# Four layers over sixteen images: attention scores without their zero blocks, mixing by 64-row halves, a third tile for the exponentials, and an altered order in the search and in the softmax of q

## The chip, the cores and the metric

The kernel runs on one core of one Trainium2 chip. The metric is the device time of one execution in microseconds (us), the median over several runs. All data are float32 unless a tile is named as bf16. The engines are TensorE (PE, with weight loads shown apart as PEld), VectorE (DVE), ScalarE (ACT), GpSimd (POOL) and SyncE (SP, which only issues transfers).

## The reference, cut to what matters

The input is 16 images of 64 x 64 positions with 256 channels. Each layer first normalizes by groups of 8 channels (`_gn`) and adds its result to its input.

```
x = x + L0(gn(x))   # nearest of 1024 codes: argmin of distances, then a lookup
x = x + L1(gn(x))   # per image row of 64 positions: sigmoid(f g^T) h
x = x + L2(gn(x))   # gate = sigmoid(sum_n x2[n] softmax_n(x0[n] x1[m])), times x
x = x + L3(gn(x))   # linear attention, 4 heads of 32, then a layer norm over channels

# L1, the part that the change touches most
f = x Wf + bf ; g = x Wg + bg ; h = x Wh + bh      # 32, 32 and 256 columns
attn = sigmoid(einsum('bhik,bhjk->bhij', f, g))    # 64 x 64 for each image row
out  = einsum('bhij,bhjo->bhio', attn, h)

# L3
q = softmax over the 32 values of a head; k = softmax over the 4096 positions
context = k v^T ; out = (context q) w_out + b_out ; layer norm over 256 channels
```

## The kernel before, in words

An image is 4096 tokens, handled in 8 chunks of 512 (`NCHUNK`, `CW`), a chunk as 4 groups of 128 tokens (`CH`). Every layer is a Python generator that emits instructions and yields a number, its share of progress. At the end of `tile_net_kernel` a list of tasks gives each generator a start and a length on a common axis where one image is one unit; a heap always advances the generator that is due next. So about five images are in flight, each in another layer, and the written order on every engine is a mixture of all layers. The framework adds the waits, and may move an instruction past others of its engine that are not ready. [...]

The stages, with the names used below:

- `stage1` (search): for each group of 128 tokens, ACT writes `nn` (L377), PE makes distances `pd` (L382), DVE adds and takes the maximum (`nd`, L389) and finds its index (`i8`, L394), and POOL issues a gather that adds the code row to the tokens `xc` (L395). `norm(ch)` prepares the next chunk: ACT normalizes (L327) and squares (L330), PE sums (`px`, L336) and turns (`pxt`, L343); `norm_rows(ch)` is one DVE copy `nx2` (L348) that `nn` needs. `back(ch)` turns the gathered tokens (PE, L357), copies them (ACT, L360) and stores them; `tokens` (L321) and `load` (L317) are issues on SP's queue. Before, `norm(ch+1)` comes after group 1 of a chunk, `norm_rows(ch+1)` and `back(ch-1)` after group 2, `tokens` and `load` after group 3.
- `layer1`: `attend(ch)` makes `fg` (PE L465, ACT L472), `h` (PE L476 and L481, ACT L485) and the scores `psc` (PE L494). A group of 128 tokens holds two image rows, so of each 128 x 128 block of scores only the two 64 x 64 blocks on its diagonal are wanted. ACT writes those into `attn`, whose other blocks were set to zero once (L497 tanh, four times for a chunk; L500 scaling, twice). `mix(ch)` multiplies `h` by the 128 x 128 `attn` (PE L509, eight products for a chunk), and DVE adds the result to `xt` (L513).
- `rows2` and `stage2` (exponentials): for 32 groups and two halves, ACT writes `ex`, 128 x 2048 exponentials (L619), and DVE multiplies and sums it in place (L622). `ex` has two tiles. A gate per token follows (L630 to L642); `gate2` applies it.
- `stage3`: for each chunk `pk` (PE L729), its exponential `kx`, `pqv` (PE L751, L755), then transposes `pkt` (L762), the transposes `pq` of the chunk before (`queries`, L717), and the softmax of q: maximum on DVE (L770), subtraction on POOL (L771), exponential on ACT (L772), sum and reciprocal on DVE (L774, L775), product on POOL (L776). After the loop `queries(7)`, then the product of context and `w_out` (PE `pw` L798, DVE `wctx` L800), and eight rounds of output, of which `form` (L817 to L823) reads the queries back from DRAM.

A float32 product appears in the trace as two passes, each with its weight load: a chunk's `mix` is 16 records of PE and 16 of PEld.

Of the kernel before, what the change touches and what calls it, by code (L numbers as in the profile page):

```python
# [16 lines left out]
P = 128  # L17
# [24 lines left out]
def kernel(  # L42
# [82 lines left out]
    def row_tile(name):  # L125
        t = const.tile([P, 2, C], BF16, name=name)
        nc.gpsimd.memset(t, 0.0)
        return t

    h_row, qv_row, x_row = row_tile("h_row"), row_tile("qv_row"), row_tile("x_row")  # L130

    def put_row(dst, v, weight, tag, plus=None):
# [11 lines left out]
        nc.scalar.copy(dst[0:PARTS, :, :], row.unsqueeze(1).to_broadcast([PARTS, 2, C]))  # L144
# [43 lines left out]
    w_src = w_qkv.rearrange("(k p) (s n) -> p k s n", p=P, s=3)  # L188


    gam = s3p.tile([P, C], F32, tag="v2", name="gam", bufs=5)
    nc.scalar.dma_start(out=gam, in_=gamma.rearrange("(o n) -> o n", o=1).to_broadcast([P, C]))

    def centred(src, name):
        t = const.tile([P, 2, C], F32, name=name)
        nc.scalar.dma_start(out=t[:, 0, :], in_=src)
        m = small.tile([P, 1], F32, tag="cen", name=f"cen_{name}")
        nc.vector.tensor_reduce(m, t[:, 0, :], AX.X, ALU.add)
        nc.vector.tensor_scalar(m, m, -1.0 / C, None, ALU.mult)
        nc.vector.tensor_scalar(t[:, 0, :], t[:, 0, :], m, None, ALU.add)  # L200
        nc.vector.tensor_tensor(t[:, 1, :], t[:, 0, :], gam, ALU.mult)
        return t

    wo2 = centred(w_out, "wo2")


    bo2 = centred(b_out.rearrange("(o n) -> o n", o=1).to_broadcast([P, C]), "bo2")
    nc.vector.tensor_scalar(bo2, bo2, float(DH ** 0.5 / HEADS), None, ALU.mult)

# [25 lines left out]

    attn = []
    for n in range(2):
        t = const.tile([P, CH, P], F32, name=f"attn_{n}")
        nc.vector.memset(t, 0.0)
        attn.append(t)  # L240
# [67 lines left out]
    def stage1(b):  # L308
# [63 lines left out]
        for ch in range(NCHUNK):  # L372
            for t in range(CH):
# [27 lines left out]
                if t == 1:  # L401
                    if ch + 1 < NCHUNK:
                        norm(ch + 1)
                        yield 2
                if t == 2:
                    if ch + 1 < NCHUNK:
                        norm_rows(ch + 1)
                    if ch > 0:
                        back(ch - 1)
                        yield 2  # L410
                if t == 3:
                    if ch + 1 < NCHUNK:
                        tokens(ch + 1)
# [10 lines left out]
    def layer1(b):  # L424
# [31 lines left out]
        hs = {}  # L456
        st2 = stats_tile(2, f"st2_{tag}")

        def attend(ch):
# [14 lines left out]
            for t in range(CH):  # L474
# [5 lines left out]
                if t % 2 == 1:  # L480
                    nc.tensor.matmul(  # L481
                        ph[:, t - 1 : t + 1, :], lhsT=ones3, rhs=h_row, start=False, stop=True, skip_group_check=True
# [5 lines left out]
            at = attn[ch % 2]  # L488
            for n in range(2):
                psc = bank(f"psc_{tag}_{ch}_{n}").rearrange("p (t i) -> p t i", i=P)  # L490
                part = slice(n * CK, (n + 1) * CK)
                for t in range(2):
                    cols = slice(t * P, (t + 1) * P)
                    nc.tensor.matmul(psc[:, t, :], lhsT=fg[part, 1, cols], rhs=fg[part, 0, cols], start=True, stop=True)  # L494
                for r in range(2):
                    rows = slice(r * ROW, (r + 1) * ROW)
                    nc.scalar.activation(at[rows, 2 * n : 2 * n + 2, rows], psc[rows, 0:2, rows], AF.Tanh, scale=0.5)  # L497
            for r in range(2):
                rows = slice(r * ROW, (r + 1) * ROW)
                nc.scalar.activation(at[rows, :, rows], at[rows, :, rows], AF.Identity, scale=0.5, bias=half[rows, :])  # L500
# [3 lines left out]
        def mix(ch):  # L504
            at = attn[ch % 2]
            po = wide(f"po_{tag}_{ch}").rearrange("p (k n) -> p k n", k=NK)
            for t in range(CH):
                for k in range(NK):
                    nc.tensor.matmul(  # L509
                        po[:, k, t * P : (t + 1) * P], lhsT=hs[ch][:, t, k * P : (k + 1) * P], rhs=at[:, t, :],  # L510
                        start=True, stop=True,
                    )
            nc.vector.tensor_tensor(xt[ch], po, xt[ch], ALU.add)  # L513
# [80 lines left out]
    def stage2(b, parts=1):  # L594
# [19 lines left out]
        for part in range(parts):  # L614
            those = range(part * NT // parts, (part + 1) * NT // parts)
            for h, (x0b, x2b) in enumerate(halves):
                for T in those:
                    ex = s2p.tile([P, TOK // 2], F32, tag="ex", name=f"ex_{tag}_{h}_{T}", bufs=2)
# [18 lines left out]
            nc.vector.reciprocal(gate, gate)  # L637
            pg = bank(f"pgt_{tag}_{part}")
# [4 lines left out]
            yield 2  # L643
# [46 lines left out]
    def stage3(b):  # L690
# [22 lines left out]
        def queries(ch):  # L713
# [4 lines left out]
            qT = s3p.tile([P, CW], F32, tag="v2", name=f"qT_{tag}_{ch}", bufs=5)  # L718
# [4 lines left out]

        for ch in range(NCHUNK):
            xt = xb.tile([P, NK, CW], F32, tag="xb", name=f"xk_{tag}_{ch}")
            nc.sync.dma_start(out=xt, in_=x3[ch])
            pk = bank(f"pk_{tag}_{ch}")
# [9 lines left out]
            kx = s3p.tile([P, CW], F32, tag="v2", name=f"kx_{tag}_{ch}", bufs=5)  # L737
# [8 lines left out]
            for pr in range(CH // 2):  # L746
# [8 lines left out]
                nc.tensor.matmul(pqv, lhsT=ones3, rhs=qv_row, start=False, stop=True, skip_group_check=True)  # L755
# [7 lines left out]
            ek = s3p.tile([P, CH, P], F32, tag="v2", name=f"ek_{tag}_{ch}", bufs=5)  # L763
# [9 lines left out]
            qd = small.tile([P, CH, HEADS], F32, tag="qd", name=f"qd_{tag}_{ch}")  # L773
# [166 lines left out]
```

## Time and profile before

| | us |
|---|---|
| median of 3 runs | 6005.67 |
| the three runs | 5981.41, 6005.67, 6006.36 |
| the profiled execution, its own time | 5985.76 |
| its span, first to last instruction | 5984.0 |
| PE busy | 5310.6 (89%) |
| DVE busy | 5132.9 (86%) |
| ACT busy | 4756.8 (79%) |
| POOL busy | 1873.7 (31%) |
| mean granted TensorE clock | 0.949 |

The busy time of an engine is the union of its records. PE's records overlap, and an isolated one lasts longer than its slot in a stream, so PE's busy share does not say that it ran at its peak. A wait is put down to the instruction whose signal came last.

### The profile page before, as it was taken

The page shows a single profiled execution, that of the slowest core. Times are in us where ns is not written, and L with a number is a line of the kernel's source. Part 1 is how long each engine was busy: PE and PEld are TensorE (multiplying, and loading weights), DVE is VectorE, ACT ScalarE, POOL GpSimd, SP SyncE. Part 2 cuts the span into 40 slices and gives each one's busy share as a digit, 9 for nine tenths or more (in the row PEclk, how much of TensorE's full clock was granted, in tenths as well). Part 3 has the DMA queues.
Part 4 walks back from the last instruction along what each step waited for, and adds up shares of the span by engine and source line. Part 5 has one row for each costly group of instructions (what it writes and reads, how often), then busy time and mean ns, then how long its engine had stood idle before and what let it go on. Part 6 is the DMA issues. An engine that isn't in the chain of part 4 may idle for free.

```text
span 5984.0 us, 73947 instructions
## 1 busy us (share of the span) xinstructions
PE 5310.6 (89%) x25167; PEld 3208.0 (54%) x25167; DVE 5132.9 (86%) x7270; ACT 4756.8 (79%) x7138; POOL 1873.7 (31%) x1314
## 2 busy tenths in 40 slices
PE   8978798989989899998989989898999989887777
PEld 3535355545556465554646556464655646464445
DVE  6589698899989899898989989898998989888862
ACT  4578597878888797888979788797988879787763
POOL 3222224233332333323333332433333333312231
PEclk9989899999999999999999999999999999998788
DMA  6453645665656657565665746566475655545543
GB/s 185 143 160 112 209 132 186 187 187 158 207 165 201 194 160 227 149 210 163 197 212 156 224 151 207 172 199 203 153 223 160 204 183 172 188 140 176 170 144 111
DMA packets 521359, 1059.10 MB, mean 177 GB/s; under 512 B 52504, under 2 KB 266392, under 8 KB 512792
## 3 DMA queue, kind: packets, MB, share of 16 engines
q1 hardware_dynamic: 406288, 885.11, 44.6%
q0 software_dynamic: 73728, 67.14, 7.8%
q10 hardware_dynamic: 40968, 102.13, 4.5%
q8 instruction: 200, 3.28, 0.2%
q14 instruction: 175, 1.43, 0.1%
HBM read 751.18 MB, written 303.04 MB: 176 GB/s over the span
## 4 chain that ended last, share of the span: by engine, by line
PE 48%; DVE 21%; ACT 15%; issue 7%; DMA 5%; POOL 4%; ACTq 0%; SPq 0%; POOLq 0%; DVEq 0%
PE pd_s L382 16%; DVE ex_s L622 10%; ACT ex_s L619 6%; PE ph_l L476 4%; PE pqv_s L751 4%; PE po_s L849 3%; DVE i_s L394 2%; PE pk_s L729 2%; PE pr_r L567 2%; DVE nd_s L389 2%; PE po_l L509 2%; POOL xc_s L395 2%; PE pvr_s L829 1%; DVE st_s L254 1%; PE pc_s L780 1%
## 5 line engine op out<-in xcount | busy, mean ns | idle before, releaser
L622 DVE CUSTOM_DVE_ANT_0 ex_s<-ex_s,x2b 128x2048 f32<-128x2048 f32 x1024 | 2369.4, 2318 | 135.9 <-ACT ex_s L619 133.5
L619 ACT ACTIVATE ex_s<-x0b,nmax_s,x_r 128x2048 f32<-128x2048 f32 x1024 | 2138.8, 2089 | 64.7 <-DVE num_s L622 55.0
L382 PE MATMUL pd_s<-e,xn_s 128*128 128x512 f32 x4096 | 2013.5, 621 | 87.6 <-DVE m L389 63.8
L395 POOL DMA_INDIRECT xc_s<-in_emb_rows,i_s x512 | 1084.0, 2117 | 1962.9 <-DVE i_s L394 1460.6
L382 PEld LDWEIGHTS pd_s<-e,xn_s 128*128 128x128 f32 x4096 | 750.6, 196 | 830.4 <-issue 655.0
L389 DVE CUSTOM_DVE_ANT_0 nd_s<-pd_s,nn_s 128x1024 f32<-128x1024 f32 x512 | 620.5, 1212 | 114.8 <-PE pd_s L382 85.4
L394 DVE FIND_INDEX8 i_s<-m,nd_s 128x8 uint32<-128x1024 f32 x512 | 623.5, 1218 | 0.0
L377 ACT ACTIVATE nn_s<-ne,nx_s 128x1024 f32<-128x1024 f32 x512 | 585.1, 1145 | 10.6 <-DVE nx_s L348 3.4
L476 PE MATMUL ph_l<-wh_l,xt_l 128*128 128x256 f32 x2048 | 534.6, 396 | 28.6 <-DVE xt_l L513 20.6
L751 PE MATMUL pqv_s<-wqv_s,xk_s 128*128 128x256 f32 x2048 | 491.9, 381 | 2.9 <-ACT xt_s L360 2.9
L476 PEld LDWEIGHTS ph_l<-wh_l,xt_l 128*128 128x128 f32 x2048 | 381.7, 194 | 155.1 <-issue 61.2
L751 PEld LDWEIGHTS pqv_s<-wqv_s,xk_s 128*128 128x128 f32 x2048 | 388.4, 191 | 130.1 <-issue 63.3
L832 POOL TENSOR_TENSOR lrs_s<-lrs_s,mhalf 128x4 f32<-128x4 f32 x128 | 187.6, 1465 | 651.5 <-ACT lrs_s L831 638.0
L849 PE MATMUL po_s<-wctx_s,qo_s 128*128 128x256 f32 x1024 | 329.4, 412 | 63.5 <-ACT y_s L852 59.8
L852 ACT ACTIVATE y_s<-po_s,lrs_s 128x256 f32<-128x256 f32 x512 | 236.0, 470 | 147.5 <-PE po_s L849 104.3
L327 ACT ACTIVATE xn_s<-xt_s,nb_n,s_n 128x512 f32<-128x512 f32 x256 | 202.4, 806 | 108.2 <-DMA xt_s<-in_xT 98.6
L776 POOL TENSOR_TENSOR qv_s<-qv_s,qd_s 128x512 f32<-128x512 f32 x128 | 167.2, 1307 | 385.3 <-DVE qd_s L775 312.8
L509 PE MATMUL po_l<-attn,h_l 128*128 128x128 f32 x2048 | 280.7, 283 | 7.3 <-DVE m L389 5.2
L509 PEld LDWEIGHTS po_l<-attn,h_l 128*128 128x128 f32 x2048 | 259.9, 195 | 45.8 <-issue 22.1
L849 PEld LDWEIGHTS po_s<-wctx_s,qo_s 128*128 128x128 f32 x1024 | 178.0, 199 | 194.5 <-ACT y_s L852 123.9
L729 PE MATMUL pk_s<-xk_s,wk_s 128*128 128x512 f32 x512 | 256.6, 623 | 0.0
L860 DVE TENSOR_TENSOR y_s<-pxo_s,y_s 128x512 f32<-128x512 f32 x256 | 174.1, 683 | 91.4 <-ACT y_s L852 91.3
(197 smaller groups left out, 7707.6 us busy)
## 6 DMA issues: line engine op xcount, KB each, us to landing
xs_s<-in_xT SPq DMA_DIRECT2D x128, 512.0 KB
xt_s<-in_xT SPq DMA_DIRECT2D x128, 512.0 KB
xc_s<-in_x SPq DMA_DIRECT2D x128, 512.0 KB
x_s<-xt_s ACTq DMA_DIRECT2D x128, 512.0 KB
xt_l<-x_s SPq DMA_DIRECT2D x128, 512.0 KB
x_l<-xt_l SPq DMA_DIRECT2D x128, 512.0 KB
xr_r<-x_l SPq DMA_DIRECT2D x128, 512.0 KB
xg_g<-x_l SPq DMA_DIRECT2D x128, 512.0 KB
```

The costliest lines, as they stand in the source:

```text
L377: nc.scalar.activation(nn, ne2, AF.Identity, bias=nx2[ch][:, t : t + 1])
L382: nc.tensor.matmul(pd[:, cols], lhsT=xn[ch][:, k, t * P : (t + 1) * P], rhs=e2[:, k, cols], start=(k == 0), stop=(k == NK - 1),)
L389: nc.vector.tensor_tensor_reduce(out=nd, in0=pd, in1=nn, scale=1.0, scalar=-3.0e38, op0=ALU.add, op1=ALU.max, accum_out=m8[:, 0:1],)
L394: nc.vector.max_index(i8, m8, nd)
L395: nc.gpsimd.indirect_dma_start(out=xc[ch][:, t, :], out_offset=None, in_=emb_rows, in_offset=bass.IndirectOffsetOnAxis(ap=i8[:, 0:1], axis=0),
L476: nc.tensor.matmul(ph[:, t, :], lhsT=X[:, k, t * P : (t + 1) * P], rhs=wh_n[:, k, :], start=(t % 2 == 0 and k == 0), stop=False, skip_grou ...
L509: nc.tensor.matmul(po[:, k, t * P : (t + 1) * P], lhsT=hs[ch][:, t, k * P : (k + 1) * P], rhs=at[:, t, :], start=True, stop=True,)
L619: nc.scalar.activation(ex, x0b, AF.Exp, bias=nmax[:, T : T + 1], scale=x01[:, T, 1:2], accum_out=den[:, h, T : T + 1])
L622: nc.vector.tensor_tensor_reduce(out=ex, in0=ex, in1=x2b, scale=1.0, scalar=0.0, op0=ALU.mult, op1=ALU.add, accum_out=num[:, h, T : T + 1],)
L729: nc.tensor.matmul(pk, lhsT=wk_n[:, k, :], rhs=xt[:, k, :], start=(k == 0), stop=(k == NK - 1))
L751: nc.tensor.matmul(pqv[:, j, :], lhsT=xt[:, k, t * P : (t + 1) * P], rhs=wqv_n[:, k, :], start=(j == 0 and k == 0), stop=False, skip_group ...
L849: nc.tensor.matmul(po[:, j, :], lhsT=qT[:, t * P : (t + 1) * P], rhs=wctx[:, 1, :], start=True, stop=True)
```

## The change

In `layer1`, `attend` makes for each of a chunk's image rows only the 64 x 64 block that is wanted: four products of 32 rows, 128 weight columns and 128 moving columns become eight of 32 rows, 64 weight columns and 64 moving columns, placed so that `psc` holds 128 x 64 for each group. ACT then needs two tanh instructions and one scaling for a chunk. The constant `attn` tiles go; `at` is a rotating tile of 128 x 4 x 64. `mix` multiplies 64 rows at a time: sixteen products of 64 rows, 128 weight columns and 64 moving columns, the two halves of a group one after the other, each half into its own bank of `po`.

`ex` gets a third tile. In `stage1` `back(ch-1)` moves from after group 2 to after group 1, `norm(ch+1)` from 1 to 2, `norm_rows(ch+1)` from 2 to 3. In `stage3` the sum, reciprocal and product of q's softmax become `normalize(ch)`, emitted at the beginning of the next chunk; `queries(7)` moves behind the making of `wctx` and `gram`; `w_out` times gamma is no longer kept, so `pw` has 256 columns and DVE multiplies `wctx` by gamma itself. The row tiles for `ones3` lose their doubled copy (read twice by a broadcast). The `v2` ring goes from 5 to 4 tiles, `wT` and `gram` share the places of `wk_n` and `ctx_bd`. The gate's PE transpose gets a yield ahead of it. `layer1` of the first image gets the length 0.2 in place of 0.35.

```diff
-        nc.scalar.copy(dst[0:PARTS, :, :], row.unsqueeze(1).to_broadcast([PARTS, 2, C]))
+        nc.scalar.copy(dst[0:PARTS, :], row)
...
                 yield 4
-                if t == 1:
-                    if ch + 1 < NCHUNK:
-                        norm(ch + 1)
-                        yield 2
-                if t == 2:
+                if t == 1 and ch > 0:
+                    back(ch - 1)
+                    yield 2
+                if t == 2 and ch + 1 < NCHUNK:
+                    norm(ch + 1)
+                    yield 2
+                if t == 3:
                     if ch + 1 < NCHUNK:
                         norm_rows(ch + 1)
-                    if ch > 0:
-                        back(ch - 1)
-                        yield 2
-                if t == 3:
-                    if ch + 1 < NCHUNK:
                         tokens(ch + 1)
...
-                        ph[:, t - 1 : t + 1, :], lhsT=ones3, rhs=h_row, start=False, stop=True, skip_group_check=True
+                        ph[:, t - 1 : t + 1, :], lhsT=ones3, rhs=twice(h_row), start=False, stop=True, skip_group_check=True
...
-            at = attn[ch % 2]
+            at = ats[ch] = s1p.tile([P, CH, ROW], F32, tag="at", name=f"at_{tag}_{ch}")
+            psc = [bank(f"psc_{tag}_{ch}_{n}").rearrange("p (t i) -> p t i", i=ROW) for n in range(2)]
+            for t in range(2):
+                for r in range(2):
+                    cols = slice(t * P + r * ROW, t * P + (r + 1) * ROW)
+                    for n in range(2):
+                        part = slice(n * CK, (n + 1) * CK)
+                        nc.tensor.matmul(
+                            psc[n][r * ROW : (r + 1) * ROW, t, :], lhsT=fg[part, 1, cols], rhs=fg[part, 0, cols],
+                            start=True, stop=True,
+                        )
             for n in range(2):
-                psc = bank(f"psc_{tag}_{ch}_{n}").rearrange("p (t i) -> p t i", i=P)
-                part = slice(n * CK, (n + 1) * CK)
-                for t in range(2):
-                    cols = slice(t * P, (t + 1) * P)
-                    nc.tensor.matmul(psc[:, t, :], lhsT=fg[part, 1, cols], rhs=fg[part, 0, cols], start=True, stop=True)
-                for r in range(2):
-                    rows = slice(r * ROW, (r + 1) * ROW)
-                    nc.scalar.activation(at[rows, 2 * n : 2 * n + 2, rows], psc[rows, 0:2, rows], AF.Tanh, scale=0.5)
-            for r in range(2):
-                rows = slice(r * ROW, (r + 1) * ROW)
-                nc.scalar.activation(at[rows, :, rows], at[rows, :, rows], AF.Identity, scale=0.5, bias=half[rows, :])
+                nc.scalar.activation(at[:, 2 * n : 2 * n + 2, :], psc[n][:, 0:2, :], AF.Tanh, scale=0.5)
+            nc.scalar.activation(at, at, AF.Identity, scale=0.5, bias=half)
...
-            po = wide(f"po_{tag}_{ch}").rearrange("p (k n) -> p k n", k=NK)
-            for t in range(CH):
-                for k in range(NK):
-                    nc.tensor.matmul(
-                        po[:, k, t * P : (t + 1) * P], lhsT=hs[ch][:, t, k * P : (k + 1) * P], rhs=at[:, t, :],
-                        start=True, stop=True,
-                    )
-            nc.vector.tensor_tensor(xt[ch], po, xt[ch], ALU.add)
+            po = wide(f"po_{tag}_{ch}").rearrange("p (r m i) -> p r m i", r=2, i=ROW)
+            for k in range(NK):
+                for t in range(CH):
+                    for r in range(2):
+                        rows = slice(r * ROW, (r + 1) * ROW)
+                        nc.tensor.matmul(
+                            po[:, r, k * CH + t, :], lhsT=h[rows, t, k * P : (k + 1) * P], rhs=at[rows, t, :],
+                            start=True, stop=True,
+                        )
+            X = xt[ch].rearrange("p k n -> p (k n)").rearrange("p (m r i) -> p m r i", r=2, i=ROW)
+            nc.vector.tensor_tensor(X, po.rearrange("p r m i -> p m r i"), X, ALU.add)
...
-                    ex = s2p.tile([P, TOK // 2], F32, tag="ex", name=f"ex_{tag}_{h}_{T}", bufs=2)
+                    ex = s2p.tile([P, TOK // 2], F32, tag="ex", name=f"ex_{tag}_{h}_{T}", bufs=3)
...
+            yield 1
             pg = bank(f"pgt_{tag}_{part}")
...
-            yield 2
+            yield 1
...
+        def normalize(ch):
+            q4 = qvs[ch][:, :, 0, :].rearrange("p t (h d) -> p t h d", d=DH)
+            qd = small.tile([P, CH, HEADS], F32, tag="qd", name=f"qd_{tag}_{ch}")
+            nc.vector.tensor_reduce(qd, q4, AX.X, ALU.add)
+            nc.vector.reciprocal(qd, qd)
+            nc.gpsimd.tensor_tensor(q4, q4, qd.unsqueeze(3).to_broadcast([P, CH, HEADS, DH]), ALU.mult)
+
         for ch in range(NCHUNK):
...
+            if ch > 0:
+                normalize(ch - 1)
             pk = bank(f"pk_{tag}_{ch}")
...
             nc.scalar.activation(qv[:, :, 0, :], qv[:, :, 0, :], AF.Exp)
-            qd = small.tile([P, CH, HEADS], F32, tag="qd", name=f"qd_{tag}_{ch}")
-            nc.vector.tensor_reduce(qd, q4, AX.X, ALU.add)
-            nc.vector.reciprocal(qd, qd)
-            nc.gpsimd.tensor_tensor(q4, q4, qd.unsqueeze(3).to_broadcast([P, CH, HEADS, DH]), ALU.mult)
...
-        queries(NCHUNK - 1)
+        normalize(NCHUNK - 1)
...
-            nc.tensor.matmul(pw, lhsT=ctx_bd, rhs=wo2, start=True, stop=True)
+            nc.tensor.matmul(pw[:, :C], lhsT=ctx_bd, rhs=wo, start=True, stop=True)
...
-            nc.vector.scalar_tensor_tensor(
-                wctx, pw.rearrange("p (s c) -> p s c", s=2), rk, bo2, op0=ALU.mult, op1=ALU.add
-            )
+            nc.vector.scalar_tensor_tensor(wctx[:, 0, :], pw[:, :C], rk, bo, op0=ALU.mult, op1=ALU.add)
+            nc.vector.tensor_tensor(wctx[:, 1, :], wctx[:, 0, :], gam, ALU.mult)
...
-            wT = wts.tile([P, NK, P], F32, tag="wT", name=f"wT_{tag}")
+            wT = wts.tile([P, NK, P], F32, tag="wk_n", name=f"wT_{tag}")
...
-            gram = wts.tile([P, P], F32, tag="gram", name=f"gram_{tag}")
+            gram = wts.tile([P, P], F32, tag="ctx_bd", name=f"gram_{tag}")
...
         yield 4
+        queries(NCHUNK - 1)
...
-        end = task("layer1", b + 1 + LAG1, LEN1 if left and b else 0.35, layer1(b), 88)
+        end = task("layer1", b + 1 + LAG1, (LEN1 if b else 0.2) if left else 0.35, layer1(b), 88)
```

## The prediction

> **What bounds the kernel now.** I read the page's busy shares first, then the windows, then who waited for whom, then the groups by form, and last the timeline around `psc` and `mix`.
>
> ```profile
> PE 5310.6 (89%) x25167; PEld 3208.0 (54%) x25167; DVE 5132.9 (86%) x7270; ACT 4756.8 (79%) x7138; POOL 1873.7 (31%) x1314
> ...
> 1200.00:4800.00 3600.00, 3305.20 (x15983) 2011.54 (x15984) 3259.26 (x4593) 3021.05 (x4535) 1185.51 (x819) 0.97 0.60 187
> 2782.00:3134.00 352.00, 325.08 (x1574) 199.09 (x1574) 318.13 (x453) 296.19 (x445) 117.49 (x82) 0.96 0.60 188
> ```
>
> The columns of the windows are PE, PEld, DVE, ACT, POOL. In the steady part an image takes 352 us: the same stall of PE (`pg_n`) recurs at 2782, 3134 and 3486 us. Of these PE is busy 325, DVE 318, ACT 296. So PE is the tightest, DVE is 7 us behind it, and no engine is full: PE's 27 us of gaps are what a change of order can win, and PE's 325 are a floor for the period.
>
> ```profile
> ACT qv_s L772 <- POOL qv_s L771: 89.8, 48, 4.4
> DVE ex_s L622 <- ACT ex_s L619: 82.3, 65, 3.2
> DVE qd_s L774 <- ACT qv_s L772: 47.0, 35, 3.0
> PE pg_n L264 <- DVE qd_s L775: 43.9, 10, 5.6
> ACT ex_s L619 <- DVE num_s L622: 29.9, 22, 2.4
> PE po_s L849 <- ACT y_s L852: 28.9, 36, 2.2
> PE px_s L336 <- ACT sq_s L330: 27.3, 14, 3.2
> PE pq_s L717 <- POOL qv_s L776: 23.4, 7, 3.8
> ```
>
> These are the waits of 1200 to 4800 us (us in total, times, longest). PE's gaps there are 3600 - 3305 = 295 us; over all PE's waits, half of that (149) ends on ACT, 113 on DVE, 23 on POOL. The longest, `pg_n`, is the statistics at the end of a search (transposes, ACT copy, DVE statistics behind an `ex` of 2.3 us): the reciprocal L775 is only the last DVE instruction ahead of it, and the change leaves that chain.
>
> **The change part by part.** All sums are against the profiled execution, 5985.8 us (span 5984.0). It lies 20 below the median of 6005.67; I carry the difference over to the median unchanged.
>
> *1. `mix` in halves, PE.*
>
> ```profile
> L509 PE MATMUL po_l<-attn,h_l 128*128 128x128 f32 x2048 | 280.7, 283 | 7.3 <-DVE m L389 5.2 <-ACT h_l L485 1.5 <-ACT attn L500 0.6
> ...
> 3016.25 0.95 PE L829 MATMUL pvr_s<-one,qz_s 128*128 128x1 f32 x8
> 3017.13 0.72 PE L494 MATMUL psc_l<-fg_l 32*128 32x128 f32 x8
> 3019.19 1.95 PE L509 MATMUL po_l<-attn,h_l 128*128 128x128 f32 x16
> ...
> 498.69 1.02 PE L382 MATMUL pd_s<-e,xn_s 128*128 128x512 f32 x2
> 499.64 0.72 PE L494 MATMUL psc_l<-fg_l 32*128 32x128 f32 x8
> 500.29 1.12 PE L382 MATMUL pd_s<-e,xn_s 128*128 128x512 f32 x2
> ```
>
> A `mix` now is 16 passes: (1.95 - 0.28 for the last one's length) / 15 = 0.112 us each. L829 moves one column only and still takes (0.95 - 0.25) / 7 = 0.10 a pass: the load of 128 weight columns alone fills the slot. The change doubles the passes to 32 and keeps 128 weight columns; only the moving columns halve. `psc` shows what the two halves can do: its eight passes use two row groups of 32 and take 0.72, that is four slots of 0.112 and the last length of 0.27, so two row groups load and multiply side by side. Then 32 passes are 16 pairs of 0.112 = 1.79 us, as before. The Trainium skill ("TensorEngine Tiling (Array Packing)", Theoretical Speedup) gives up to twofold for a contraction of at most 64: by that rule 0.9 us would go from each of 128 mixes, -115 us. The L829 row speaks against it, and so I take nothing.
>
> The same page (Key Properties) says that a switch of the tiling mode drains TensorE, which speaks against the change. The row: from 498.69, two slots of L382 (0.43 each, the start-to-start time within L382) end at 499.55, `psc` starts at 499.64; its four pairs would need 0.45 and the next L382 starts after 0.65; and within that one the second pass follows after 0.53, not 0.43. The excursion costs 0.09 + 0.20 + 0.10 = 0.39 us beyond its slots. A `mix` had no such switch and gets one: 128 x 0.39 = +50 us of PE. Without the rule and the row it would be 0. Bounds: if loads of 64 rows took half, 128 x (0.39 - 0.9) = -65; if the halves ran one after the other, 128 x (0.39 + 1.79) = +279. I take +50, since `psc` is the same construction.
>
> *2. Other PE work.* `psc` gets 64 weight and 64 moving columns and four tiles of the array; its four rounds of 0.112 may halve: 128 x -0.22 = -29, or 0; I take -25 (the column-tiled L465 runs four tiles side by side as well). `pw` loses 256 of 512 columns: 2 passes x 0.215 x 16 images = -7. PE in all: +50 - 25 - 7 = +18, of which 92% (PE's busy share, 1200 to 4800) reach the time: **+16**.
>
> *3. ACT.*
>
> ```profile
> L497 ACT ACTIVATE attn<-psc_l 64x128 f32<-64x128 f32 x512 | 138.2, 270 | 70.6 <-PE psc_l L494 59.3 <-issue 2.8
> L500 ACT ACTIVATE attn<-attn,half 64x256 f32<-64x256 f32 x256 | 129.5, 506 | 6.3
> ```
>
> The elements of a partition stay the same, the instructions halve: a chunk saves 2 x 270 + 506 = 1046 ns, 128 chunks 134 us; 48 row copies of 3x512 (565 ns) become 3x256 (356 ns, row L142), -10. ACT loses 144 of 4757 us. ACT isn't the bound: it idles 579 of 3600 us. What it gives is that fewer waits end on it. Scaled from 3600 us to all images (352 us each, 16) PE's waits on ACT are 230. A fall from 84% to 81% busy should shorten its queueing by about a fifth: **-45**; bounds 0 (DVE, as full, takes its place) and -144.
>
> *4. Third `ex` tile.* No instruction is added. ACT's waits for DVE at L619 are 55 us in all, DVE's for ACT at L622 133. A pair costs DVE 2318 + 82 and ACT 2089 + 190 ns, so on average DVE is the slower and the buffer smooths only. **-12**, bounds 0 and -60. When ACT runs ahead, other ACT work behind those exponentials comes later by up to 2.3 us; that is in the bound.
>
> *5. q's softmax.* DVE stands 70.6 us for L772's exponential at L774 (57 times); a yield later it is done. POOL's product moves as well, and PE's `pq`, which waits for it 51.7 us already, gets one yield less. The steady 3.8 us of each image are of the first chunk: POOL stands 9.2 us after its all-reduce (row `POOL qv_s L771 <- issue`), three gathers queue, then L776. That remains. **-12**; bounds -50 and +50. `queries(7)` behind `wctx` costs nothing elsewhere: its transposes were ahead of `pw` and are now ahead of the first `form`, which in steady state has three other layers beside it; uncovered, at the end, 0.7 PE and 0.6 ACT and a store.
>
> *6. Order in the search.* SP's load L317 waits 401 us in all for the store of the chunk two before (94 times, up to 8.4); ACT waits 98.6 at L327 for such loads. With `back` a group earlier the store is done when SP comes to L317, and L321, the tokens (421 us on `back`'s transposes), goes sooner; what is behind them on SP's queue too. Against that, PE's transposes come nearer to the gathers (they wait 33.6 us at 330 to 1200 us), and `nn` of the next chunk now stands right behind `nx2` in the written order: DVE copy, ACT 1145 ns, DVE L389. If nothing fills that, DVE loses 1.15 us in 128 chunks, +147; if the loads' waits went whole, -60. I take **0**. The PE work moved is equal.
>
> *7. First image.* In 0 to 330 us DVE is busy 198 of 330, PE 297; at 300 to 600 us DVE 276 of 300. Image 0's exponentials start 0.15 units earlier: 0.15 x (2369 + 84) / 16 = 23 us of DVE work move into DVE's idle part. Half of it: **-12**, bounds 0 and -23.
>
> *8. Ends, small things.* The yield before the gate's transpose frees PE of 9 us in the last image, `queries(7)` of 3 to 9 us in the last ones, by waits at the end where PE isn't full: **-8**, bounds 0 and -20. `wctx`: one DVE instruction of 745 ns becomes two of some 450, +2 in all. The fourth `v2` tile and the shared places hold tiles whose readers are a chunk or a stage away: 0; if not, a wait of a store of some 4 us in 16 images, +64.
>
> Sum: +16 - 45 - 12 - 12 + 0 - 12 - 8 = **-73 us**: 5913 for the profiled execution, **5933** for the median.
>
> **The rivals.**
>
> *The halves don't run side by side (slower).* Place: L509's successor on PE. Two row groups of 64 rows would then take 32 slots of 0.112, 1.79 us more for each mix; 128 x 1.79 x 0.92 = +211, less 73: **6144**. It decides from 0.62 us more than my 2.2 + 0.28 us in a mix (73 / 128 / 0.92): a mix of over 3.1 us in the timeline. Against it speaks `psc` with groups of 32; for it, that no row shows groups of 64.
>
> *The search's shorter lead is the new wait (slower).* 147 of section 6, PE behind it: -73 + 147 = **6080**. For it: DVE is 90% busy; against: the framework fills with other stages' work, and L377 waited only 3.4 us on `nx2`.
>
> *The gaps are dealt anew.* ACT's 144 us go into its idle time and DVE's 90% becomes the wait: only sections 2, 7 and 8 count, +16 - 12 - 8 = -4: **6002**. For it: DVE is within 7 us of PE.
>
> *More comes.* ACT's saving passes whole, the waits of 4 and 5 go by half (-94): +16 - 144 - 94 / 2 - 20, about -150 after a part that PE's floor takes: **5850**.
>
> **How the numbers follow.** My forecast 0.50 (own range 5875 to 5990), more 0.17, dealt anew 0.19, halves in series 0.07, search 0.07. A measurement of this kernel tells about 0.5%, 30 us, from no change: 5976 to 6036. Faster by more than that: 0.17 and nearly all of 0.50, 0.66. Within: 0.19 and a little of the forecast and of the search, 0.22. Slower: 0.12. The range is 5840 to 6040: outside it are the two slow cases' upper parts (0.10) and some of the fastest (0.05).
>
> **What would show it.** `mix`: 32 PE records over 2.0 to 2.4 us, starts in pairs; 3.4 or more is the first rival, 1.4 the skill's twofold. ACT busy near 4613. Tanh 256 times at 270 ns, scaling 128 times at 506. L774's wait for L772 below 20 us, L317's for the store near 0, the sum of PE's gaps in an image from 27 to about 21 us. A new large DVE or ACT wait for `nn` or `nx2` is the second rival. Wrong would be a period of an image of 352 us or more.

## The result: 1% faster, the forecast total, but not in the forecast place

| | before | after |
|---|---|---|
| median, us (same chip, 4 runs each) | 6005.56 | 5935.15 |
| range of the runs | 5981.41 to 6006.36 | 5928.44 to 5938.41 |
| span of the profiled execution | 5984.0 | 5926.7 |
| mean granted TensorE clock in it | 0.949 | 0.941 |

The ratio is 0.9903, 95% interval 0.9888 to 0.9919. Forecast were 5933 us. The busy times on the page after:

```profile
PE 5337.4 (90%) x28239; PEld 3211.1 (54%) x28239; DVE 5121.1 (86%) x7282; ACT 4570.8 (77%) x6754; POOL 1939.4 (33%) x1314
```

ACT lost 186 us and PE gained 27. The windows after (PE, PEld, DVE, ACT, POOL, then PE's granted clock): the steady part as shown of before, then ten images from the start of the product `pw` of image 1 to that of image 11, then the rest, in which the pipeline empties.

```profile
1200.00:4800.00 3600.00, 3348.08 (x17976) 2026.67 (x17975) 3247.06 (x4608) 2903.20 (x4285) 1264.32 (x820) 0.95 0.60 187
1483.80:5005.60 3521.80, 3288.48 (x17640) 1994.01 (x17640) 3168.98 (x4506) 2846.34 (x4208) 1244.66 (x810) 0.95 0.60 187
5005.60:5926.70 921.10, 754.14 (x3906) 498.49 (x3904) 716.54 (x1001) 665.85 (x1069) 252.68 (x204) 0.90 0.50 165
```

The same two stretches of before:

```profile
1488.60:5015.40 3526.80, 3248.91 (x15722) 1980.39 (x15721) 3183.10 (x4496) 2960.58 (x4450) 1177.02 (x810) 0.97 0.61 187
5015.40:5984.00 968.60, 773.95 (x3598) 511.23 (x3597) 714.68 (x998) 689.99 (x1104) 255.36 (x203) 0.88 0.48 157
```

Ten images took 3526.8 us and now take 3521.8: the period of an image is 352.2 us, as good as unchanged. Of the 57 us of the span 5 came before image 1's `pw`, 5 in those ten images, and 48 in the end. Yet PE's gaps in the ten images did shrink, from 278 to 233 us (3526.8 - 3248.9, 3521.8 - 3288.5). PE's busy time grew by 40 instead. The clock explains all of that: 0.97 became 0.95, the time at half clock in the ten images rose from 212 to 320 us, and half of that rise is 54 us.

The attention's own groups after:

```profile
L506 PE MATMUL po_l<-at_l,h_l 64*128 64x64 f32 x4096 | 318.5, 297 | 46.2 <-DVE xt_l L511 42.7 <-DVE m L384 3.0 <-ACT at_l L494 0.4
L488 PE MATMUL psc_l<-fg_l 32*64 32x64 f32 x2048 | 81.9, 236 | 8.5 <-ACT kx_s L746 3.7 <-ACT y_s L857 3.3 <-ACT qv_s L764 1.5
L494 ACT ACTIVATE at_l<-at_l,half 128x256 f32<-128x256 f32 x128 | 64.8, 507 | 0.6
L493 ACT ACTIVATE at_l<-psc_l 128x128 f32<-128x128 f32 x256 | 59.9, 273 | 26.3 <-PE psc_l L488 23.0 <-PE pkt_s L770 2.5 <-ACT at_l L493 0.4
```

`mix` is dearer by 38 us (318.5 against 280.7), `psc` cheaper by 35 (117.0 before). ACT's two rows fell from 268 to 125 us. The largest waits of interest, 1200 to 4800 us:

```profile
SPq L312 <- DMA x_s<-xt_s: 350.0, 62, 8.5
...
DVE nd_s L384 <- ACT nn_s L372: 61.8, 43, 7.3
...
PE po_l L506 <- DVE xt_l L511: 42.7, 11, 4.6
PE px_s L331 <- ACT sq_s L325: 36.0, 37, 2.8
PE pr_r L565 <- DMA xr_r<-x_l: 34.3, 16, 3.9
...
DVE ex_s L620 <- ACT ex_s L617: 28.7, 31, 2.1
...
DVE qd_s L726 <- ACT qv_s L780: 10.9, 13, 1.6
```

Of PE's waits the 43.9 us of `pg_n` at the end of a search are gone (5.0 are left); in their place PE waits for the tokens `xt` that layer 1 adds to. DVE waits less for exponentials (82.3 before) and for q's (47.0), but now waits 62 us for `nn`.

**Busy, but half as useful.** The timeline of PE after, a stretch without a gap (start us, us, instructions):

```profile
1536.71 0.70 PE L854 MATMUL po_s<-wctx_s,qo_s 128*128 128x256 f32 x2
1537.24 0.95 PE L834 MATMUL pvr_s<-one,qz_s 128*128 128x1 f32 x8
1538.12 0.88 PE L506 MATMUL po_l<-at_l,h_l 64*128 64x64 f32 x10
1538.93 0.46 PE L488 MATMUL psc_l<-fg_l 32*64 32x64 f32 x16
1539.32 2.04 PE L506 MATMUL po_l<-at_l,h_l 64*128 64x64 f32 x22
```

and the windows around it:

```profile
1533.40:1536.80 3.40, 3.40 (x14) 1.80 (x12) 3.25 (x5) 3.26 (x5) 1.07 (x1) 1.00 0.17 61
1536.80:1540.20 3.40, 3.40 (x53) 3.20 (x52) 3.40 (x4) 1.46 (x5) 1.58 (x2) 1.00 0.95 254
1540.20:1547.00 6.80, 6.80 (x25) 4.60 (x23) 5.41 (x10) 6.36 (x8) 0.00 (x0) 0.50 0.66 239
```

From 1536.8 to 1540.2 us PE is busy for all of 3.40 us, and directly after it the granted clock is 0.50 for 6.8 us. What fills the first stretch are mostly records that ask little of the array: one moving column (`pvr`), 64 rows and 64 moving columns (`mix`), 32 rows and 64 moving columns (`psc`). This gave the theory that most of the experiments test: *the clock theory*, that halving the moving columns of `mix` at an unchanged slot lowers the array's work per unit of time, and that the granted clock follows this work, not PE's busy time.

### The profile page after: what moved, and what is told of

Same layout as the page of the kernel before. It is cut to its first block, busy times and chain, and to the rows that moved or that the text cites. A ratio compares the mean times of both kernels' runs of the same rounds, so it can differ in the third digit from the quotient of the medians.

```text
span 5926.7 us, 79561 instructions
## 1 busy us (share of the span) xinstructions
PE 5337.4 (90%) x28239; PEld 3211.1 (54%) x28239; DVE 5121.1 (86%) x7282; ACT 4570.8 (77%) x6754; POOL 1939.4 (33%) x1314
## 4 chain that ended last, share of the span: by engine, by line
PE 48%; DVE 16%; ACT 12%; DMA 7%; issue 6%; POOL 4%; ACTq 0%; SPq 0%; POOLq 0%; DVEq 0%
PE pd_s L377 15%; DVE ex_s L620 6%; ACT ex_s L617 5%; PE ph_l L468 5%; PE pqv_s L759 3%; PE po_s L854 3%; PE pk_s L737 3%; PE po_l L506 2%; PE pr_r L565 2%; DMA xr_r<-x_l 2%; DVE i_s L389 2%; POOL qv_s L779 2%; PE pvr_s L834 1%; PE pz_s L826 1%; DMA qo_s<-qd_s 1%
## 5 line engine op out<-in xcount | busy, mean ns | idle before, releaser
L390 POOL DMA_INDIRECT xc_s<-in_emb_rows,i_s x512 | 1058.1, 2067 | 2063.9 <-DVE i_s L389 1466.8
L506 PE MATMUL po_l<-at_l,h_l 64*128 64x64 f32 x4096 | 318.5, 297 | 46.2 <-DVE xt_l L511 42.7
L506 PEld LDWEIGHTS po_l<-at_l,h_l 64*128 64x128 f32 x4096 | 286.5, 206 | 108.5 <-DVE xt_l L511 48.9
L779 POOL TENSOR_TENSOR qv_s<-qv_s,qm_s 128x512 f32<-128x512 f32 x128 | 232.7, 1818 | 312.3 <-DVE qm_s L778 181.7
L728 POOL TENSOR_TENSOR qv_s<-qv_s,qd_s 128x512 f32<-128x512 f32 x128 | 199.8, 1561 | 304.6 <-DVE qd_s L727 252.9
L737 PE MATMUL pk_s<-xk_s,wk_s 128*128 128x512 f32 x512 | 269.6, 650 | 0.0
```

Source lines behind the costliest of these rows:

```text
L390: nc.gpsimd.indirect_dma_start(out=xc[ch][:, t, :], out_offset=None, in_=emb_rows, in_offset=bass.IndirectOffsetOnAxis(ap=i8[:, 0:1], axis=0),
L506: nc.tensor.matmul(po[:, r, k * CH + t, :], lhsT=h[rows, t, k * P : (k + 1) * P], rhs=at[rows, t, :], start=True, stop=True,)
L737: nc.tensor.matmul(pk, lhsT=wk_n[:, k, :], rhs=xt[:, k, :], start=(k == 0), stop=(k == NK - 1))
```

## The experiments

All were timed against the kernel before on the same chip. The ratios carry the comparisons; medians of different sets of runs are some us apart for the kernel before as well. "Half-clock time" is the sum of the stretches with a granted clock of 0.5 in 1200 to 4800 us of the profiled execution. The table has it first, then, per image, the ten periods from `pw` to `pw`, of which PE's busy time and gaps are the parts. (Some expectations count a stretch by its start, which gives 287 for e1.) These four columns are of one execution each, and not always of a typical one: those of the changed kernel, e1, e4, e7 and e10 are the fastest of their runs, those of e2, e6 and e9 the slowest. Where medians and profiles differ, the ratios count.

| kernel | ratio [95%] | half-clock us of 3600 | period | busy | gaps |
|---|---|---|---|---|---|
| before | 1 | 226 | 352.7 | 324.9 | 27.8 |
| after | 0.9903 [0.9888, 0.9919] | 341 | 352.2 | 328.8 | 23.3 |
| e1 attention only | 0.9945 [0.9929, 0.9961] | 282 | 353.8 | 326.1 | 27.7 |
| e2 old attention, two `ex` | 1.0137 [1.0123, 1.0152] | 287 | 364.0 | 328.7 | 35.3 |
| e3 wide moving | 0.9859 [0.9841, 0.9878] | 212 | 347.2 | 323.8 | 23.4 |
| e4 two `ex` | 1.0069 [1.0057, 1.0082] | 393 | 360.6 | 331.6 | 28.9 |
| e5 old search | 1.0052 [1.0034, 1.0070] | 451 | 360.9 | 335.5 | 25.4 |
| e6 old q | 0.9877 [0.9856, 0.9899] | 331 | 351.1 | 328.7 | 22.4 |
| e7 old length | 0.9880 [0.9859, 0.9900] | 322 | 351.1 | 327.9 | 23.2 |
| e9 all old order | 0.9999 [0.9990, 1.0008] | 393 | 356.3 | 332.8 | 23.5 |
| e10 wide, old length | 0.9826 [0.9806, 0.9846] | 204 | 347.5 | 324.1 | 23.4 |
| e11 e1, wide | 0.9931 [0.9913, 0.9949] | 191 | 349.7 | 325.0 | 24.7 |
| e12 e5, wide | 0.9899 [0.9880, 0.9918] | 251 | 352.7 | 329.0 | 23.8 |
| e13 e10, `pvr` wide | 0.9895 [0.9870, 0.9921] | 239 | 350.4 | 325.6 | 24.8 |

In every row PE's busy time less half of its own half-clock time is 312 to 317 us per image (before: 324.9 - 21.2 / 2 = 314.3; after: 328.8 - 32.0 / 2 = 312.8, by the ten images' own half-clock time). So an image's period is that floor, half the half-clock time, and the gaps. The kernels with wide products lie 2 to 4 us above their partners in this floor (e3 315.2).

**e1: the new attention alone**, in the kernel before, with its order and two `ex` tiles.

> The kernel before with the attention of layer 1 alone changed (small score blocks, two tanh and one scaling, mix in halves); order, ex tiles and the rest as before. My prediction's terms for it: +16 (PE) - 40 (ACT, without the row copies) = about -25, so 5980. The rival that the traces suggest (an image takes 352.6 us before and 352.2 after in the steady part, while PE gets half its clock for 341 of 3600 us in place of 225): the halves cost PE as much as ACT's saving gives or more, so 6005 to 6050, with a granted clock below 0.94.

It took 5962.03 us (0.9945), 18 less than the prediction's terms say and outside the rival's range. The new attention as a whole costs no time. But the gaps of an image stayed at 27.7: ACT's saved instructions shortened none of PE's steady waits in this order, and the period even rose by 1.1 us, with 56 us more at half clock. The gain lies outside the ten images: they begin 15 us earlier, and what follows them is 29 us shorter.

**e2 and e4: the third `ex` tile, and the attention in the new order.** e4 is the changed kernel with `bufs=2`; e2 has the old attention besides.

```diff
-                    ex = s2p.tile([P, TOK // 2], F32, tag="ex", name=f"ex_{tag}_{h}_{T}", bufs=3)
+                    ex = s2p.tile([P, TOK // 2], F32, tag="ex", name=f"ex_{tag}_{h}_{T}", bufs=2)
```

> The changed kernel with the old attention (128 x 128 blocks with zeros, mix in full rows) and two ex tiles, since a third one has no room beside it. To be held against e4_ex_two, which differs by the attention alone. Prediction's terms: the old attention is slower by about 25. Rival: it is equal or faster by up to 50, its granted clock in the steady part about 0.97 and an image there about 348 us, because the gain of the whole change comes from order and the end, and the halves eat the rest.

> The changed kernel with two ex tiles again. My term for the third tile was -12, so 5947. Rival (steady part held by PE): nothing in the steady part, at most some us in the end where DVE and ACT carry the last exponentials, 5935 to 5945; the waits of DVE for ACT at the ex product go from 45 us back to about 130.

e2 took 6082.89 us and e4 6038.51, which is eight times the forecast 12 above the changed kernel and outside its rival's range. From e2 to e4 the attention brings 0.0068, some 41 us, here through the gaps (35.3 to 28.9), while half-clock time rises by 106 us and takes much back. From e4 to the changed kernel the third tile brings 0.0166, 100 us: gaps 28.9 to 23.3, the rest clock. The steady windows of e4, for the DVE column above all:

```profile
1200.00:4800.00 3600.00, 3303.13 (x17506) 1989.17 (x17507) 3217.54 (x4510) 2843.55 (x4191) 1251.05 (x808) 0.95 0.59 182
```

With two tiles the new order runs at 182 GB/s and DVE 3218 us busy, with three at 187 and 3247.

**e9: all of the old order**, with the new attention and three tiles: search, q, length and the gate's yield as before.

> The changed kernel with all of the order as before (search, q's softmax, first image, gate's yield), so new attention, small tiles and three ex tiles alone. To be held against e1_attn_only (new attention, old order, two ex tiles: 5962) and e4_ex_two (new order, two tiles: 6038). Prediction's terms: 5962 less 12 for the third tile = 5950. Rival A: the new order costs 76 us whatever the tiles, then 5935 - 76 = 5860. Rival B: the third tile only takes away what the new order broke, then it gives nothing here: 5962 within 10.

It took 5993.77 us over 22 runs, which none of the three expectations had. The gaps fall again, from e1's 27.7 to 23.5 us, but the ratio rises from 0.9945 to 0.9999, 32 us, and the mean clock falls (median of the runs 0.942 for e1, 0.934 here). The profiles show 111 us more at half clock and a period longer by 2.5; e1's is of its fastest run and e9's of its slowest, so these two overstate it. So a third tile that gains 100 us in the new order comes with a loss of 32 in the old one. That this loss is the tile's own is not shown: e9 differs from e1 in the small tile edits too, the shorter `v2` ring among them.

Over the 22 runs, with nothing re-ordered, time and clock go together: from 5978.02 us at a mean clock of 0.936 to 6010.96 at 0.930, a line through all has 4.0 us (plus or minus 1.5) for each 0.001. As 0.001 is 12 us at half clock, this is 6 us of PE work at most. The kernel before gives 2.2 us over its 27 runs on the same chip and 5.2 over 11 on another, so how much of the clock's loss reaches the time is not settled, nor can such a line tell which of the two drives the other.

**e5: the search's old order** in the changed kernel.

```diff
-                if t == 1 and ch > 0:
-                    back(ch - 1)
-                    yield 2
-                if t == 2 and ch + 1 < NCHUNK:
-                    norm(ch + 1)
-                    yield 2
-                if t == 3:
+                if t == 1:
+                    if ch + 1 < NCHUNK:
+                        norm(ch + 1)
+                        yield 2
+                if t == 2:
                     if ch + 1 < NCHUNK:
                         norm_rows(ch + 1)
+                    if ch > 0:
+                        back(ch - 1)
+                        yield 2
+                if t == 3:
+                    if ch + 1 < NCHUNK:
                         tokens(ch + 1)
```

> The changed kernel with the order of the search as before (norm after group 1, back and norm_rows after group 2). My term was 0: 5935 within 10. Rival from the traces (DVE waits for nn at the nd row 82 us after the change, 14 before; PE for the gathers 57 and 35): the new order costs and the loads' waits (ACT 99 us before, 25 after) don't pay for it, then 5880 to 5915. If the loads' waits paid: 5950 to 5980.

6021.56 us, 1.0052 against 0.9903: this order costs 0.0149, 89 us, outside all three ranges. Only some 2 us of the 8.7 that it adds to each image are gaps; the busy time makes the rest, at 451 us of half clock. The long stall at the end of a search is back as well: PE waits 50.3 us for `pg_n` in 1200 to 4800 us, 43.9 before the change, 5.0 after it. It is the search's order that removes it.

**e6 and e7: q's softmax, and the first image's length, as before.**

```diff
-        end = task("layer1", b + 1 + LAG1, (LEN1 if b else 0.2) if left else 0.35, layer1(b), 88)
+        end = task("layer1", b + 1 + LAG1, LEN1 if left and b else 0.35, layer1(b), 88)
```

> The changed kernel with sum, reciprocal and product of q's softmax in their own chunk and queries(7) ahead of wctx, as before. My term was -12, so 5947. Rival: the steady part doesn't move (352 us for an image), and only the last images, where nothing else covers the chain, get slower: 5940 to 5970, all of it after 5000 us.

> The changed kernel with the first image's layer1 spread over 0.35 as before. My term was -12, so 5947. Rival: image 0 reaches its last stage 34 us earlier after the change, but image 1 only 5 us, so that nothing is left: 5935 within 8.

Medians 5925.64 and 5913.95 us, both below every expectation. Neither edit of the change brings anything that can be measured; both intervals overlap that of the changed kernel, and both old forms lie on the faster side of it. In e6 the stretch after image 11's `pw` is 18 us longer and the period 1.1 shorter.

**e3: wider moving operands**, the direct test of the clock theory. In 12 of 16 products of `mix` the moving operand takes the next group's 64 columns as well; the product after it overwrites them. The slot is set by the weight load, so this should cost PE nothing.

```diff
+                        m, n = k * CH + t, 2 if t + 1 < CH else 1
                         nc.tensor.matmul(
-                            po[:, r, k * CH + t, :], lhsT=h[rows, t, k * P : (k + 1) * P], rhs=at[rows, t, :],
+                            po[:, r, m : m + n, :], lhsT=h[rows, t, k * P : (k + 1) * P], rhs=at[rows, t : t + n, :],
```

> The changed kernel, but 12 of a chunk's 16 products in mix move 128 columns in place of 64; the second 64 of each are overwritten by the next product, so the output is the same. If a pass is held by its weight load (0.112 us) this costs nothing. If the lower clock of the changed kernel comes from the halves' low activity, the granted clock in the steady part goes from 0.95 back towards 0.97 and the time to about 5885 to 5910. If the clock falls for another reason (gaps of PE), 5935 within 10 and the clock stays. If passes are held by their moving columns: PE busy at the mix grows by 0.9 us in each of 128, up to 6040.

Median 5909.22 us, at the upper end of what the clock theory expects (5885 to 5910). Its group of `mix` and its steady window:

```profile
L507 PE MATMUL po_l<-at_l,h_l 64*128 64x128 f32 (+1 forms) x4096 | 315.2, 289 | 39.7 <-DVE xt_l L512 26.2
```

```profile
1200.00:4800.00 3600.00, 3346.44 (x18151) 2015.22 (x18152) 3303.88 (x4672) 2942.54 (x4337) 1271.57 (x830) 0.97 0.62 189
```

With three quarters of the products moving twice the columns, `mix` is no dearer (315.2 against 318.5 us on its row; one that runs at full clock without a break takes 1.93 us from its first start to that of the next product, in both kernels), the clock is back at 0.97, the gaps stay at 23.4, and the period falls to 347.2. Useless columns made the kernel faster.

**e10 to e13: the same edit elsewhere.** A single such run could be a lucky order, so the edit was put on three other orders; e13 adds 32 equal moving columns to `pvr`, which had one.

```diff
-                nc.tensor.matmul(pv[:, t : t + 1], lhsT=prod[:, t * P : (t + 1) * P], rhs=one, start=True, stop=True)
+                nc.tensor.matmul(pv[:, t, 0:32], lhsT=prod[:, t * P : (t + 1) * P], rhs=ones32, start=True, stop=True)
```

> The changed kernel with two edits that were each tried alone: the mix products move 128 columns where a next one overwrites the second 64, and the first image's layer 1 keeps its length 0.35. Clock theory (the moved columns keep the granted clock up, and the length is a matter of its own): the two gains add, 26 + 21 us, so about 5890, at half clock some 210 us of 1200 to 4800. Order theory (each of the two runs only drew another order of instructions, worth some 20 us either way): about 5915, anywhere in 5895 to 5940, with a time at half clock that may be anything from 210 to 340 us.

> The kernel before with the new attention alone, and the mix products moving 128 columns. Clock theory: time at half clock in 1200 to 4800 us falls from the 287 us of the same kernel with 64 columns to some 210, PE's busy time by half of that, 40 us, over the whole run about 50: 5962 becomes 5910 to 5935. Order theory: half-clock time stays within 250 to 320 and the time near 5962, between 5945 and 5985.

> The changed kernel with the search's old order, and the mix products moving 128 columns. With 64 columns this order had 451 us at half clock in 1200 to 4800 us and took 6022. Clock theory: at least 130 us less at half clock (320 or under), so 65 us or more less PE time there and 5940 to 5970 in all: most of what the search's order seemed to be worth was the clock. Order theory: half-clock time stays over 400, and the time stays within 6000 to 6040.

> The previous combination (128 moving columns in mix, length 0.35), and the variance products of layer 3 (pvr, 1024 records that load 128 weight columns and move 1) move 32 equal columns instead of 1. Their slot is set by the load, so PE's busy time grows by 0 to 10 us. Clock theory: a little less half-clock time still, 180 to 210 us of 1200 to 4800, and 5875 to 5890. Order theory: no fall, 5900 to 5930.

Medians 5884.29, 5954.04, 5933.61 and 5935.88 us; e10 went as the clock theory expected, e12 gained 6 us more than its range. Half-clock time fell in all four pairs: 341 to 212 (e3), 322 to 204 (e10), 282 to 191 (e11), 451 to 251 (e12). The ratio fell in all four, by 0.0044, 0.0054, 0.0014 and 0.0153; in three of them the intervals of the pair lie apart; e11's and e1's overlap. The steady windows of e5 and of e12:

```profile
1200.00:4800.00 3600.00, 3334.35 (x17518) 2016.57 (x17516) 3207.07 (x4508) 2850.85 (x4191) 1203.85 (x807) 0.94 0.58 182
```

```profile
1200.00:4800.00 3600.00, 3341.97 (x17985) 2021.88 (x17985) 3280.97 (x4605) 2911.03 (x4286) 1242.50 (x819) 0.97 0.59 187
```

PE is busy for as long in both (3334 and 3342 us), but e12 gets through 17985 matmuls in it and e5 through 17518. So of the 0.0149 that the search's order seemed worth, 0.0040 is left once `mix` moves 128 columns (e12 against e3): the clock was most of it.

e11 missed its expected time, which lies in the order theory's range (5945 to 5985), though its half-clock time does not: its ten images take 42 us less than e1's, but they begin 25 us later and its end is 17 us longer. Why is not known. Its row of `mix` also rose by 30 us, in e12 by 15:

```profile
L507 PE MATMUL po_l<-at_l,h_l 64*128 64x64 f32 x4096 | 292.9, 281 | 9.5 <-DVE m L383 5.9
```

```profile
L508 PE MATMUL po_l<-at_l,h_l 64*128 64x128 f32 (+1 forms) x4096 | 323.3, 286 | 8.3 <-DVE m L383 4.7
```

(e1, then e11.) An unbroken `mix` takes 1.93 us in these as well, so it is not the product itself; what makes the row longer is open.

e13 is a miss of the clock theory, and the order theory's "no fall" came true: it is slower than e10 by 0.0069, 41 us, with the intervals apart, and has 239 us at half clock, not less than e10's 204. The slot of `pvr` was still 112 ns, gaps rose by 1.4 us per image, and the rest is not explained; the order, dealt anew, may be all of it.

e10 is the fastest: 0.9826 of before, against 0.9903 for the changed kernel, and the intervals lie apart. Its busy line:

```profile
PE 5276.6 (90%) x28239; PEld 3170.1 (54%) x28239; DVE 5123.2 (87%) x7282; ACT 4571.0 (78%) x6754; POOL 1928.5 (33%) x1314
```

The same 28239 matmuls as in the changed kernel take 61 us less of PE.

## Why the prediction was right, and where it was not

*Section 1, the halves side by side: confirmed.* A `mix` of 32 records takes 2.0 to 2.1 us at full clock (the 30 of this timeline, after):

```profile
3013.22 2.00 PE L506 MATMUL po_l<-at_l,h_l 64*128 64x64 f32 x30
3015.14 0.70 PE L854 MATMUL po_s<-wctx_s,qo_s 128*128 128x256 f32 x2
```

Starts come in pairs 6 to 7 ns apart, every 112 ns: load-bound, the first rival dead. The twofold that the prediction quotes and sets aside did come, over halves that run one after the other; but the old `mix`, zeros included, filled all rows already, so against it nothing is won. The switch was mis-sized. At full clock, between products that use all rows, entering and leaving each cost 0.09 us more than before (L382's start to that of `mix` 0.52 after 0.43, the last start of `mix` to the next product 0.20 after 0.11), and first to last start is 1.73 us after 1.67: 0.24 us for a `mix`, at most 31 us for 128, where 0.39 and 50 were taken. Its row costs 38 us more, with more half clock, and 12 in e1.

*Section 2: right in kind.* `psc` -35 (forecast -25), `pw` 20.0 to 14.5 us (forecast -7); its four tiles start within 20 ns, as those of L465 did before. The three rows add up to -3 us, not +18, in spite of more half clock.

*Section 3: the busy time right, its worth wrong.* ACT's durations, summed over all records, fell by 143.6 us (forecast 144; the page's 186 is of the union, since its records overlap more). For that -45 were taken, as shorter waits of PE in steady state. e1 shows no shorter gap; in the new order, e2 to e4, 6.4 us of gaps per image go. What ACT's time is worth depends on the order around it, and a share of all its waits could not tell that.

*Section 4, the third tile: the largest error of size.* Forecast -12 with a bound of -60; measured some -100 in the new order; in the old one +32, the small tile edits included. The reasoning, that a buffer "smooths only", was right about what it does. But 4.2 to 5.6 us of gaps per image went with it.

*Section 5, q's softmax: half right.* DVE's wait for q's exponential at the sum fell nearly as forecast, from 70.6 to 20.4 us over the run (below 20 was the sign). But nothing was held up by it: e6 without it is no slower.

*Section 6, the search: the mechanism wrong, the sum of 0 wrong.* SP's wait for the store did not vanish; it grew, to 350 us in the steady part, where before had

```profile
SPq L317 <- DMA x_s<-xt_s: 223.1, 56, 7.1
```

The second rival's wait came too: DVE stands 62 us for `nn` (before 6.5). Still the new order is worth 89 us against the old one in this kernel, mostly by the clock. And of PE's longest wait, `pg_n`, the prediction said that the change leaves its chain; the new order all but ended it (5.0 us, and 50.3 with the old order in e5).

*Section 7: not seen.* e7 with the old length is no slower.

*Section 8, the ends: the sign right, far too small.* The stretch after image 11's `pw` fell by 48 us where -8 was forecast, 28 of them gaps and 20 PE busy time (773.95 to 754.14), which half clock alone would explain (233 to 177 us, half of it 28). In the kernels with all old order it is 940 to 969 us, in e6 939, in the others 914 to 943. The gate's yield was not tried alone.

*What was missing.* The prediction named a period of 352 us or more as the sign of being wrong, and 352.2 it is. It read PE's gaps rightly (27 to about 21 us forecast, 27.8 to 23.3 measured) and then took PE's 325 us of busy time as a floor. It is none: 10.6 us of it were half-clock loss, and they became 16.0. That the total came out within 3 us is luck, a sum of errors: a steady gain that the clock took, and a gain at the end of 48 us where 8 were forecast.

*What the clock follows.* From the trace each stretch of 3.413 us (the grid on which the granted clock changes) was given two numbers: PE's busy share, and the array's work: for each record rows x columns / 16384 x moving columns x 0.84 ns (430 ns for 512 columns, L382's slot; half of it for the bf16 products, whose next start follows after 216 ns), spread over the record, over 3413 ns. A `mix` has about 0.96 before and 0.48 after; with products of less beside it a stretch falls below 0.4. The stretch from 1536.8 us shown above has 0.35, the next one, at half clock, 0.37, and the one after it 0.50; then the full clock is back. Over before, after and the twelve experiments, 1200 to 4800 us:

| array work in a stretch | followed by half clock |
|---|---|
| under 0.3 | 865 of 1085 |
| 0.3 to 0.4 | 336 of 635 |
| 0.4 to 0.5 | 0 of 1006 |
| 0.5 and more | 0 of 12024 |

The Trainium skill ("TensorE: Matmul & The Clock Gate", Part 1, What's actually happening) lets the gate follow how busy PE has been lately. Here that is not enough: of the stretches in which PE was busy for over 90%, those with work of 0.4 or more were followed by half clock in 0 of 11413 cases, those with less in 199 of 421. Stretches with PE busy for under 70% are 103 before and 104 after; those with work under 0.4 rose from 94 to 133, and in e3 they are 102. By busy time the changed kernel should have kept before's clock; by the array's work it had to lose some of it. Low work makes half clock possible and does not settle it: of the busy stretches under 0.4, 20 of 37 led to it in the changed kernel and 1 of 16 in e3.

The loss also lies where the halves are. Stretches in which half of a `mix` or more starts:

| `mix` | followed by half clock |
|---|---|
| 128 rows (before, e2) | 5 of 177 |
| halves, 64 columns (seven kernels) | 166 of 585 |
| halves, mostly 128 columns (five kernels) | 32 of 398 |

It is 26 of 85 in the changed kernel and 8 of 83 in e3, and falls in the three other pairs too (24 to 11, 12 to 1, 26 to 7), so it does not hang on one order. The first table is a correlation; the wide products, which change the work and not the slot, are the experiment behind it.

*What stays open.* Every edit also deals the order of all layers anew, and e6, e7 and e13 show moves of 15 to 40 us of which no part could be tied to the edit. Worths of that size, and the split of the end's 48 us, are not settled. The 48 us at the end are located by the traces and tied to no edit, except that the attention alone (e1) has 29 of them. Nor is it settled why the search's old order meets so many more low stretches.

## What to carry to other kernels

When PE sets the period, read its busy time together with the granted clock: period = PE work at full clock + half of the half-clock time + gaps. Cutting a product's moving columns below what its weight load hides saves nothing and may cost clock. If the slot is free, filling it is worth a trial: for `mix` it paid in three of four orders clear of noise, for `pvr` it did not. A third buffer, or any change of order, is judged by gaps and clock apart, for both times that this one came in, the gaps fell, and the time went 100 us down in one order and 32 up in another.

## What the runs showed of the hardware

- Half clock directly after 3.40 us in which PE was busy for all of 3.40, where most records have 64 rows and 64 moving columns, 32 rows and 64 moving columns, or one moving column (1536.8 to 1547.0 us).
- Array work of 0.4 or more in 3.413 us, by the count above: never followed by half clock (0 of 13030 stretches); under 0.4: 1201 of 1720.
- Twice the moving columns at the same cost: an unbroken `mix` at full clock takes 1.93 us to the next product's start with 64 columns and with 64 and 128, and half-clock time falls by 129 us of 3600 (e3).
- Two groups of 64 rows load and multiply side by side, pairs of starts 6 to 7 ns apart every 112 ns: the load of 128 weight columns at 64 rows is no shorter than at 128 (0.112 us in both).
- A `mix` on groups of 64 rows between products on all rows: 0.09 us more to enter and 0.09 to leave than a `mix` on all rows.
